# Remaining rows of the experts in blocks of 64 rows, and each tile's results behind its own products

## The chip, the cores and the metric

The kernel runs on one core of one Trainium2 chip, as one launch. The metric is the device time of that launch in microseconds (us), as the median of several executions. The engines are named as in the profile: PE (TensorE) multiplies matrices, PEld is PE's loading of weights, DVE (VectorE) and ACT (ScalarE) work on elements, POOL (GpSimd) here mostly issues indirect DMAs, SP (SyncE) issues plain ones. Work passes between engines through semaphores.

## The reference, cut to what matters

Two layers work on x, of 2 x 2048 tokens with 256 features. The first is a gated linear attention plus a quantised linear map. The second adds, to a normalised input, an attention with 16 heads and a mixture of 8 experts. The change concerns the mixture alone:

```python
logits = xf @ gate_W.T                     # xf: 4096 tokens x 256
pi = _sinkhorn(-logits)                    # 4096 x 8
_, top_idx = jax.lax.top_k(pi, 2)          # two experts for each token
g = jnp.einsum('nd,efd->enf', xf, W_gate)  # 1024 hidden features
u = jnp.einsum('nd,efd->enf', xf, W_up)
y = jnp.einsum('enf,edf->end', jax.nn.silu(g) * u, W_down)
for k in range(2):
    out = out + y[top_idx[:, k], n_ar] * pi[:, k:k + 1]
```

Each token needs only its own two experts, so 8192 pairs of token and expert are to be computed. With the fixed inputs the reference sends 1047, 977, 950, 1003, 1054, 1044, 1029 and 1088 tokens to the eight experts.

## The kernel before, in words

The first layer is worked through in strips of 512 tokens (to about 430 us of the span). Then come the attention of the second layer, with the routing as background work on DVE (to about 894 us), and last the experts' stage.

**Routing.** `Routing.steps` ranks the experts for each token and counts the tokens of each expert. The rows of an expert are laid out in a table in DRAM (`table`) in blocks. `number` is how many whole blocks of 256 rows (`BS`) an expert gets: its count plus 127, divided by 256, rounded down. Where rows remain beyond those, `half` is 1 and the expert gets one block of 128 rows as well. With the counts above each expert gets four whole blocks; three of them don't fill these, and five experts have 23, 30, 20, 5 and 64 rows left, each in a block of 128. `end` sums blocks over the experts, `start` and `away` turn places into rows of the table, `ended`, `expert`, `mine` and `wrow` tell for each block whose it is. `sends` scatters the tokens' rows into the table; rows without a token hold a spare row that adds to a spare part of the output.

**Blocks run.** The program always runs the same list: 32 whole blocks (`FULLS`) and 5 short ones (`HALVES`), the short ones at places 8, 15, 22, 29 and 36 of the 37. If the counts call for more, a flag (`over`, then `c.special` and `c.more`) makes a later branch run all blocks that are not in the list.

**A block** (class `Block`) has these steps:
- `load`: two gathers on POOL (L2146) of the expert's weights, `wgateup` with 2 MB and `wdown` with 1 MB, and one load of its rows on SP's queue (L2162). They are traced two blocks ahead.
- `open_rows`: transposes of the rows on PE into `x_ps` (L2184), a copy to `xT` on ACT (L2188), and three small steps on DVE that take the rows' weights `wt` and the places `to`.
- `hidden`: for each of 8 slices of 128 hidden features, four products into `h_ps` (L2206): the expert's weights, 128 x 128, are the stationary operand and the block's rows the moving one. ACT's silu gives `sg` (L2211), and DVE multiplies it into `hT` (L2212; the profile calls that room `larger`).
- `add_rows`: for each tile of 128 rows 8 products into `y_ps` (L2222): here the rows of `hT` are the stationary operand and 256 columns of `wdown` the moving one. Then, for each tile, DVE multiplies by `wt` and adds half of a bias (L2227; its output `y` appears as `va`), and POOL adds the rows to the output with an indirect DMA (L2231).

All is fp32, and a fp32 product leaves two weight loads and two product records in the trace. The two tiles of a whole block share one PSUM tile of 128 x 512 (`y_ps`, in a pool of one buffer); `h_ps` and `x_ps` draw on seven others.

**Order.** `Experts.pieces` writes the order: for block n the loads of block n+2, `hidden` of n, `open_rows` of n+1, then `add_rows` of n-1. In the last block `add_rows` of the block before stands behind the first quarter of `hidden`. The framework's planner then orders each engine's queue by its own reckoning of when each instruction is ready, with program order as priority. `keep_in_program_order` holds single instructions (the transposes, the row loads, two of the small DVE steps) behind what was traced on their engine before. The framework sets all semaphores.

Of the kernel before, what the change touches and what calls it, by code (L numbers as in the profile page):

```python
# [56 lines left out]
I32 = mybir.dt.int32  # L57
AF = mybir.ActivationFunctionType
ALU = mybir.AluOpType
# [3 lines left out]
P = 128  # L63
B, N, E = 2, 2048, 256
# [18 lines left out]
NE, FF = 8, 1024  # L83
NFC = FF // P
BS = 256
NC = BS // P
NFULL = (2 * B * N + NE * (BS // 2 - 1)) // BS
NHALF = NE
NBLK = NFULL + NHALF
ROWS = NFULL * BS + NHALF * BS // 2  # L90
FULLS, HALVES = 2 * B * N // BS, 5
SPARE = B * N
RW = E + NE + 1
SINKHORN_ITERS = 20
# [121 lines left out]
@with_exitstack  # L216
def two_layers(ctx: ExitStack, tc: tile.TileContext, a: dict, out: bass.AP):
    nc = tc.nc
    const = ctx.enter_context(tc.tile_pool(name="const", bufs=1))

    def load(name, shape, view=None, eng=None, dt=F32):
        t = const.tile(shape, dt, tag=name, name=name)
        (eng or nc.sync).dma_start(out=t, in_=view if view is not None else a[name])
        return t

    c = SimpleNamespace()
    c.ident = load("ident", [P, P])
# [12 lines left out]
    c.wrow = const.tile([P, NBLK], I32, tag="wrow", name="wrow")  # L240
    c.half_bias = const.tile([P, E], F32, tag="half_bias", name="half_bias")

    dram = ctx.enter_context(tc.tile_pool(name="dram", bufs=1, space=bass.MemoryType.DRAM))
    c.table = dram.tile([ROWS, RW], F32, tag="table", name="table")
    c.normed = dram.tile([B * N, E], F32, tag="normed", name="normed")
    c.normed_v = c.normed.rearrange("(t p) e -> p t e", p=P)
    c.qk = dram.tile([2, 2, P, B * N], F32, tag="qk", name="qk")
    c.v = dram.tile([B * N, VW], F32, tag="v", name="v")
    c.x_in = a["x"].rearrange("b n e -> (b n) e").rearrange("(t p) e -> p t e", p=P)
    c.out_v = out[0 : B * N, :].rearrange("(t p) e -> p t e", p=P)  # L250

    blocks = list(range(FULLS))
    for i in range(HALVES):
        blocks.insert(FULLS - 6 * i, NFULL + i)
    usual_way(tc, a, out, c, blocks)

    def where(flag):
        return tc.If(nc.values_load(flag[0:1, 0:1], min_val=0, max_val=1) > 0)

    with where(c.special):  # L260
        with where(c.more):
            layer1_experts(tc, a, out, c, [b for b in range(NBLK) if b not in blocks])
        with where(c.general):
            general_way(tc, a, out, c)
# [35 lines left out]
def general_way(ctx, tc, a, out, c):  # L300
# [16 lines left out]
    nc.vector.memset(c.half_bias, 0.0)  # L317
    layer1_experts(tc, a, out, c, range(NBLK))


class Fill:
# [1603 lines left out]
class Routing:  # L1925
# [3 lines left out]
    def __init__(self, nc, vector, pool, a, c):  # L1929
# [24 lines left out]
    def steps(self, pool, psum, pi):  # L1954
# [5 lines left out]
        nc, vector = self.nc, self.vector  # L1960
# [64 lines left out]
        count = upto[:, NT - 1, :]  # L2025
# [2 lines left out]
        vector.tensor_scalar(number, count, float(BS // 2 - 1), None, ALU.add)  # L2028
        vector.tensor_scalar(number, number, BS.bit_length() - 1, None, ALU.logical_shift_right)
        blocks = tile_("blocks", [P, 2, NE])  # L2030
        full, half = blocks[:, 0, :], blocks[:, 1, :]
        vector.tensor_copy(full, number)
        in_full = tile_("in_full", [P, NE])
        vector.tensor_scalar(in_full, full, float(BS), None, ALU.mult)
        vector.tensor_tensor(half, count, in_full, ALU.is_gt)
        yield
        end = blocks
        for step in (1, 2, 4):
# [5 lines left out]
            end = more  # L2044
# [3 lines left out]
        vector.tensor_scalar(start, start, float(BS), None, ALU.mult)  # L2048

        away = tile_("away", [P, NE])  # L2050
        vector.tensor_tensor(away, end[:, 1, :], half, ALU.subtract)
        vector.scalar_tensor_tensor(away, end[:, 0, :], -2.0, away, ALU.mult, ALU.add)
        vector.tensor_scalar(
            away, away, float(BS // 2), float(NFULL * BS), ALU.mult, ALU.add
        )
        yield
        shape = [P, NT, NE]
# [10 lines left out]
        for to, mark in zip(self.places, (first, second)):  # L2068
            own = tile_("own", [P, NT, NE], tag="sk_beaten")
# [6 lines left out]

        ended = tile_("ended", [P, NBLK, NE], tag="sk_equal")
        for n, bs in enumerate((slice(0, NFULL), slice(NFULL, NBLK))):
# [14 lines left out]
        vector.tensor_scalar(row, expert, float(P), self.pidx, ALU.mult, ALU.add)  # L2093
        vector.tensor_copy(self.c.wrow, row)
        over = self.over
        for n, done in enumerate((FULLS, HALVES)):
            vector.tensor_scalar(
                over[:, n : n + 1], end[0:1, n, NE - 1 :], float(done), None, ALU.is_gt
            )
# [33 lines left out]
class Block:  # L2133


    def __init__(self, e, n, b):
        self.e, self.n, self.b = e, n, b
        self.tiles = NC if b < NFULL else NC // 2
        self.rows = self.tiles * P
        self.first = b * BS if b < NFULL else NFULL * BS + (b - NFULL) * BS // 2  # L2140

    def gather(self, name):

# [14 lines left out]
        self.wd = self.gather("wdown").rearrange("p (c d) -> p c d", c=NFC)  # L2158

    def load_rows(self):  # L2160
        self.xb = self.e.rooms("xb", self.n, [P, NC, RW])[:, 0 : self.tiles, :]
        load = self.e.nc.sync.dma_start(  # L2162
            out=self.xb,
            in_=self.e.c.table[self.first : self.first + self.rows, :].rearrange(
                "(c p) r -> p c r", p=P
            ),
        )
        self.e.tc.keep_in_program_order(load)
# [6 lines left out]
    def open_rows(self):  # L2175


        nc, rooms, n, xb, keep = (
            self.e.nc, self.e.rooms, self.tiles, self.xb, self.e.tc.keep_in_program_order
        )  # L2180
        ps = rooms("x_ps", self.n, [P, 2 * BS]).rearrange("p (e r) -> p e r", e=2)
        for e in range(2):
            for c in range(n):
                keep(nc.tensor.transpose(  # L2184
                    ps[:, e, c * P : (c + 1) * P], xb[:, c, e * P : (e + 1) * P], self.e.c.ident
                ))
        self.xT = rooms("xT", self.n, [P, 2, BS])
        nc.scalar.copy(self.xT[:, :, 0 : self.rows], ps[:, :, 0 : self.rows])  # L2188
        by = rooms("by", self.n, [P, NC, NE])[:, 0:n, :]
        keep(nc.vector.tensor_tensor(  # L2190
            by, xb[:, :, E : E + NE],
            self.e.c.mine[:, self.b : self.b + 1, :].to_broadcast([P, n, NE]), ALU.mult,
        ))
        self.wt = rooms("wt", self.n, [P, NC])
        nc.vector.tensor_reduce(self.wt[:, 0:n], by, AX.X, ALU.add)
        self.to = rooms("to", self.n, [P, NC], I32)
        keep(nc.vector.tensor_copy(self.to[:, 0:n], xb[:, :, E + NE]))

    def hidden(self):
# [14 lines left out]
                yield  # L2214

    def add_rows(self):
        nc, out = self.e.nc, self.e.out
        ps = self.e.rooms("y_ps", self.n, [P, NC * E]).rearrange("p (c d) -> p c d", c=NC)
        y = self.e.rooms("y", self.n, [P, NC, E])
        for c in range(self.tiles):  # L2220
            for fc in range(NFC):
                nc.tensor.matmul(  # L2222
                    ps[:, c, :], lhsT=self.hT[:, fc, c * P : (c + 1) * P], rhs=self.wd[:, fc, :],
                    start=fc == 0, stop=fc == NFC - 1,
                )
        for c in range(self.tiles):
            nc.vector.scalar_tensor_tensor(  # L2227
                y[:, c, :], ps[:, c, :], self.wt[:, c : c + 1], self.e.c.half_bias,
                ALU.mult, ALU.add,
            )  # L2230
            nc.gpsimd.indirect_dma_start(  # L2231
                out=out, out_offset=bass.IndirectOffsetOnAxis(ap=self.to[:, c : c + 1], axis=0),
                in_=y[:, c, :], in_offset=None, compute_op=ALU.add,
            )


# [50 lines left out]
def _constants():  # L2287
    f32 = np.float32
    c = {"ident": np.eye(P, dtype=f32)}
# [21 lines left out]
    to = ((s <= t) * 1 - (s <= 63)).astype(f32)  # L2311
# [3 lines left out]
    own = np.zeros((P, HR), f32)  # L2315
# [4 lines left out]
    c["spare"] = np.zeros((P, RW), f32)  # L2320
    c["spare"][:, E + NE] = SPARE + np.arange(P)
    c["number"] = (np.arange(NT)[None, :, None] * P + np.arange(P)[:, None, None]).astype(f32)
    own = np.concatenate([np.arange(NFULL), np.arange(NHALF)])
    c["bidx"] = np.broadcast_to(own[None, :, None], (P, NBLK, NE)).astype(f32)
    c["eidx"] = np.broadcast_to(np.arange(NE)[None, :], (P, NE)).astype(f32)
    c["before"] = np.tile((np.arange(NE)[None, :] < np.arange(NE)[:, None]).reshape(1, -1), (P, 1)).astype(f32)
# [122 lines left out]
```

## Time and profile before

| | us |
|---|---|
| median of 3 runs | 1642.38 (1642.37 to 1642.56) |
| the profiled execution, its own time | 1642.09 |
| its span in the profile | 1640.3 |
| PE busy | 1583.8 (97%) |
| DVE busy | 730.3 (45%) |
| ACT busy | 743.9 (45%) |
| POOL busy | 391.2 (24%) |
| experts' stage, from the first `h_ps` record | 893.5 to the end |
| mean share of the clock granted to PE | 0.989 |

The span counts from the first to the last profiled instruction; the device time has some 1.8 us more around it. "Busy" is the union of an engine's instructions. The timeline and the chain give starts and lengths in us from the span's start. In the timeline a product's record includes its latency, so that records overlap; the chain shows the time by which each moved the end.

### The profile page before, as it was taken

Reading aid. Unit: us, or ns where it says so; the run is one execution under the profiler, and the core shown is the slowest. Engines: PE = TensorE matmul, PEld = TensorE weight load, DVE = VectorE, ACT = ScalarE, POOL = GpSimd, SP = SyncE. Lnnn points to the kernel's source line nnn. Section 1 sums busy time; section 2 is a strip of 40 time slices with the busy share of each in tenths; the row PEclk is TensorE's granted clock in tenths of the full one; section 3 lists DMA queues with packets and bytes.
Section 4 is the critical chain, followed back from the end, with each engine's and each line's share of the span. In section 5 each row is a group of like instructions: output and inputs, shape, how many; then the busy total and the mean of one; then the engine's idle time right before and its main releaser. Section 6 shows DMA issues by size and latency. Waiting matters only on the chain.

```text
span 1640.3 us, 33123 instructions
## 1 busy us (share of the span) xinstructions
PE 1583.8 (97%) x13786; PEld 1297.9 (79%) x13786; DVE 730.3 (45%) x2274; ACT 743.9 (45%) x1445; POOL 391.2 (24%) x350
## 2 busy tenths in 40 slices
PE   7789999999999999999999999999999999999996
PEld 4556676667688887888888888988898898888886
DVE  7888676664478866444353222222222222222221
ACT  4344554653688888998987211111111111111110
POOL 4333222211200003233331122222222232222221
PEclk9999999999899999999999999999999999999998
DMA  9710111313540402621126555555565565556531
GB/s 268 187 38 29 54 53 43 93 45 80 149 57 3 84 13 66 142 65 62 58 97 246 180 177 177 180 183 174 180 205 198 164 215 195 171 170 196 177 90 19
DMA packets 82511, 204.42 MB, mean 125 GB/s; under 512 B 8624, under 2 KB 64304, under 8 KB 71728
## 3 DMA queue, kind: packets, MB, share of 16 engines
q0 software_dynamic: 24944, 138.33, 26.0%
q1 hardware_dynamic: 56304, 62.71, 14.2%
q8 instruction: 110, 1.80, 0.5%
q10 hardware_dynamic: 1104, 1.18, 0.2%
q14 instruction: 49, 0.40, 0.1%
HBM read 152.26 MB, written 49.92 MB: 123 GB/s over the span
## 4 chain that ended last, share of the span: by engine, by line
PE 86%; DVE 9%; POOL 2%; ACT 1%; DMA 1%; issue 1%; POOLq 0%; SPq 0%; DVEq 0%; ACTq 0%
PE h_ps L2206 29%; PE y_ps L2222 14%; PE sc L1801 12%; PE o_ps L1823 10%; PE vf_ps L533 3%; PE y_ps L533 3%; PE f_ps L1785 2%; PE tr L583 2%; PE vg_ps L533 2%; PE qk_ps L533 1%; PE g_ps L533 1%; PE q_ps L533 1%; PE o_tr L1758 1%; PE o_ds_ps L533 1%; PE x_ps L2184 1%
## 5 line engine op out<-in xcount | busy, mean ns | idle before, releaser
L2206 PE MATMUL h_ps<-va,qk 128*128 128x256 f32 (+1 forms) x2368 | 484.5, 365 | 0.0
L2206 PEld LDWEIGHTS h_ps<-va,qk 128*128 128x128 f32 x2368 | 425.6, 190 | 53.6 <-issue 0.3
L1807 ACT ACTIVATE pt<-sc,shift 128x512 f32<-128x512 f32 (+3 forms) x687 | 403.8, 704 | 52.3 <-ACT pt L1807 27.1
L2211 ACT ACTIVATE sg<-h_ps 128x256 f32<-128x256 f32 (+1 forms) x296 | 109.2, 369 | 600.5 <-PE h_ps L2206 592.9
L2212 DVE TENSOR_TENSOR larger<-sg,h_ps 128x256 f32<-128x256 f32 (+1 forms) x296 | 119.2, 403 | 359.1 <-ACT sg L2211 359.1
L1801 PE MATMUL sc<-qk 32*128 32x128 f32 (+6 forms) x3916 | 222.5, 336 | 1.6 <-PE norm_ps L533 1.1
L1801 PEld LDWEIGHTS sc<-qk 32*128 32x128 f32 x3916 | 184.1, 186 | 35.3 <-ACT pt L1807 17.0
L1823 PE MATMUL o_ps<-pt,va 128*32 128x128 f32 (+6 forms) x3916 | 188.3, 319 | 3.4 <-DVE o_sb L114 3.4
L1823 PEld LDWEIGHTS o_ps<-pt,va 128*32 128x32 f32 x3916 | 140.6, 110 | 34.3 <-issue 9.6
L2231 POOL DMA_INDIRECT out<-va,to x69 | 109.9, 1592 | 211.0 <-DMA out<-va,to 85.4
L114 DVE TENSOR_TENSOR pt<-pt,keepmask 128x128 f32<-128x128 f32 (+3 forms) x546 | 119.7, 276 | 73.7 <-ACT pt L1807 71.8
L2222 PE MATMUL y_ps<-qk,larger 128*128 128x256 f32 x560 | 124.6, 379 | 0.1
L2227 DVE SCALAR_TENSOR_TENSOR va<-y_ps,wt,half_bias 128x256 f32<-128x256 f32 x69 | 30.4, 479 | 208.5 <-PE y_ps L2222 208.5
L2222 PE MATMUL y_ps<-larger 128*128 128x256 f32 x544 | 120.4, 379 | 0.0
L2222 PEld LDWEIGHTS y_ps<-qk,larger 128*128 128x128 f32 x560 | 104.7, 190 | 13.8 <-DVE larger L2212 0.5
L2222 PEld LDWEIGHTS y_ps<-larger 128*128 128x128 f32 x544 | 102.0, 190 | 13.1
L2116 POOL DMA_INDIRECT table<-rows,place x64 | 67.7, 1057 | 186.0 <-DMA table<-rows,place 149.4
L2146 POOL DMA_INDIRECT qk<-in_wgateup,wrow x37 | 36.7, 991 | 190.4 <-PE h_ps L2206 157.7
L533 PE MATMUL vf_ps<-qk,xnT 128*128 128x512 f32 x128 | 59.2, 617 | 0.0
L533 PEld LDWEIGHTS vf_ps<-qk,xnT 128*128 128x128 f32 x128 | 24.4, 196 | 29.6 <-issue 27.3
L114 DVE COPY o_sb<-o_ps 128x256 f32<-128x256 f32 x64 | 26.9, 422 | 42.1 <-PE o_ps L1823 41.8
L2146 POOL DMA_INDIRECT qk<-in_wdown,wrow x19 | 18.4, 968 | 110.2 <-PE y_ps L2222 83.6
(248 smaller groups left out, 1712.2 us busy)
## 6 DMA issues: line engine op xcount, KB each, us to landing
xb<-table SPq DMA_DIRECT2D x32, 265.0 KB
qk<-qk SPq DMA_DIRECT2D x32, 256.0 KB
qk<-qk SPq DMA_DIRECT2D x64, 128.0 KB
table<-spare SPq DMA_DIRECT2D x3, 2120.0 KB
va<-v SPq DMA_DIRECT2D x4, 1208.0 KB
v<-v SPq DMA_DIRECT2D x8, 574.0 KB
normed<-xn SPq DMA_DIRECT2D x8, 512.0 KB
rows<-normed POOLq DMA_DIRECT2D x16, 256.0 KB, 3.3
```

What stands on the lines that cost most here:

```text
L114: return lambda *a, **k: self.tc.keep_in_program_order(begin(*a, **k))
L533: tc.keep_in_program_order(nc.tensor.matmul(*args, **kwargs))
L1801: nc.tensor.matmul(scs[r][:, at : at + q1 - q0], lhsT=heads[rows, 1, kb * P : (kb + 1) * P], rhs=heads[rows, 0, qt * QT + q0 : qt * QT + q ...
L1807: nc.scalar.activation(pt[:, r, 0:width], scs[r][:, 0:width], AF.Exp, bias=shift)
L1823: nc.tensor.matmul(o_ps[r * HR : (r + 1) * HR, to + q0 : to + q1], lhsT=values[b, way][:, kb, h * VC : h * VC + HR], rhs=pt[:, r, at : at ...
L2116: self.nc.gpsimd.indirect_dma_start(out=self.c.table, in_=rows[:, n, :], in_offset=None, out_offset=bass.IndirectOffsetOnAxis(ap=to[:, 2 * ...
L2146: e.nc.gpsimd.indirect_dma_start(out=w, out_offset=None, in_=e.a[name], in_offset=bass.IndirectOffsetOnAxis(ap=e.c.wrow[:, self.b : self.b ...
L2206: nc.tensor.matmul(ps[:, j, rows], lhsT=self.wgu[:, j, c, f * P : (f + 1) * P], rhs=self.xT[:, c, rows], start=c == 0, stop=c == 1,)
L2211: nc.scalar.activation(sg, ps[:, 0, rows], AF.Silu)
L2212: nc.vector.tensor_tensor(self.hT[:, f, rows], sg, ps[:, 1, rows], ALU.mult)
L2222: nc.tensor.matmul(ps[:, c, :], lhsT=self.hT[:, fc, c * P : (c + 1) * P], rhs=self.wd[:, fc, :], start=fc == 0, stop=fc == NFC - 1,)
L2231: nc.gpsimd.indirect_dma_start(out=out, out_offset=bass.IndirectOffsetOnAxis(ap=self.to[:, c : c + 1], axis=0), in_=y[:, c, :], in_offset= ...
```

## The change

Blocks for remaining rows have 64 rows (`SB`) in place of 128, and an expert may have none, one or two of them: `small` is 1 where rows remain, and 2 where more than 64 do. There are up to 16 such blocks in place of 8 (`NBLK` goes from 43 to 51); the list that always runs still has 32 whole blocks and 5 short ones (`SMALLS`). The table has the same number of rows. A short block's tiles take 64 partitions, its transposes, `hidden` and `add_rows` work on 64 rows. In `add_rows` the second loop over the tiles is gone: DVE's step and the scatter of a tile stand behind the tile's own 8 products, ahead of the products of the next tile.

```diff
-NHALF = NE
-NBLK = NFULL + NHALF
-ROWS = NFULL * BS + NHALF * BS // 2
-FULLS, HALVES = 2 * B * N // BS, 5
+SB = 64
+NSMALL = 2 * NE
+NBLK = NFULL + NSMALL
+ROWS = NFULL * BS + NSMALL * SB
+FULLS, SMALLS = 2 * B * N // BS, 5
...
-        vector.tensor_tensor(half, count, in_full, ALU.is_gt)
+        vector.tensor_tensor(small, count, in_full, ALU.is_gt)
+        two = tile_("two", [P, NE])
+        vector.scalar_tensor_tensor(two, in_full, float(SB), count, ALU.add, ALU.is_lt)
+        vector.tensor_tensor(small, small, two, ALU.add)
...
-        vector.tensor_tensor(away, end[:, 1, :], half, ALU.subtract)
-        vector.scalar_tensor_tensor(away, end[:, 0, :], -2.0, away, ALU.mult, ALU.add)
+        vector.tensor_tensor(away, end[:, 1, :], small, ALU.subtract)
+        vector.scalar_tensor_tensor(
+            away, end[:, 0, :], -float(BS // SB), away, ALU.mult, ALU.add
+        )
...
-        self.tiles = NC if b < NFULL else NC // 2
-        self.rows = self.tiles * P
-        self.first = b * BS if b < NFULL else NFULL * BS + (b - NFULL) * BS // 2
+        self.tiles, self.p = (NC, P) if b < NFULL else (1, SB)
+        self.rows = self.tiles * self.p
+        self.first = b * BS if b < NFULL else NFULL * BS + (b - NFULL) * SB
...
                 keep(nc.tensor.transpose(
-                    ps[:, e, c * P : (c + 1) * P], xb[:, c, e * P : (e + 1) * P], self.e.c.ident
+                    ps[:, e, c * P : c * P + p], xb[:, c, e * P : (e + 1) * P],
+                    self.e.c.ident[0:p, 0:p],
                 ))
...
         for c in range(self.tiles):
             for fc in range(NFC):
                 nc.tensor.matmul(
-                    ps[:, c, :], lhsT=self.hT[:, fc, c * P : (c + 1) * P], rhs=self.wd[:, fc, :],
+                    ps[0:p, c, :], lhsT=self.hT[:, fc, c * P : c * P + p], rhs=self.wd[:, fc, :],
                     start=fc == 0, stop=fc == NFC - 1,
                 )
-        for c in range(self.tiles):
             nc.vector.scalar_tensor_tensor(
-                y[:, c, :], ps[:, c, :], self.wt[:, c : c + 1], self.e.c.half_bias,
+                y[0:p, c, :], ps[0:p, c, :], self.wt[:, c : c + 1], self.e.c.half_bias[0:p, :],
                 ALU.mult, ALU.add,
             )
             nc.gpsimd.indirect_dma_start(
                 out=out, out_offset=bass.IndirectOffsetOnAxis(ap=self.to[:, c : c + 1], axis=0),
-                in_=y[:, c, :], in_offset=None, compute_op=ALU.add,
+                in_=y[0:p, c, :], in_offset=None, compute_op=ALU.add,
             )
```

More of the change, by code (lines that the diff above doesn't have):

```diff
@@ L252, in two_layers @@
     blocks = list(range(FULLS))
-    for i in range(HALVES):
+    for i in range(SMALLS):
         blocks.insert(FULLS - 6 * i, NFULL + i)
@@ L2030, in steps @@
         blocks = tile_("blocks", [P, 2, NE])
-        full, half = blocks[:, 0, :], blocks[:, 1, :]
+        full, small = blocks[:, 0, :], blocks[:, 1, :]
         vector.tensor_copy(full, number)
@@ L2050, in steps @@
         away = tile_("away", [P, NE])
-        vector.tensor_tensor(away, end[:, 1, :], half, ALU.subtract)
-        vector.scalar_tensor_tensor(away, end[:, 0, :], -2.0, away, ALU.mult, ALU.add)
+        vector.tensor_tensor(away, end[:, 1, :], small, ALU.subtract)
+        vector.scalar_tensor_tensor(
+            away, end[:, 0, :], -float(BS // SB), away, ALU.mult, ALU.add
+        )
         vector.tensor_scalar(
-            away, away, float(BS // 2), float(NFULL * BS), ALU.mult, ALU.add
+            away, away, float(SB), float(NFULL * BS), ALU.mult, ALU.add
         )
@@ L2095, in steps @@
         over = self.over
-        for n, done in enumerate((FULLS, HALVES)):
+        for n, done in enumerate((FULLS, SMALLS)):
             vector.tensor_scalar(
@@ L2160, in load_rows @@
     def load_rows(self):
-        self.xb = self.e.rooms("xb", self.n, [P, NC, RW])[:, 0 : self.tiles, :]
+        self.xb = self.e.rooms("xb", self.n, [P, NC, RW])[0 : self.p, 0 : self.tiles, :]
         load = self.e.nc.sync.dma_start(
@@ L2164, in load_rows @@
             in_=self.e.c.table[self.first : self.first + self.rows, :].rearrange(
-                "(c p) r -> p c r", p=P
+                "(c p) r -> p c r", p=self.p
             ),
@@ L2175, in open_rows @@
     def open_rows(self):
-        nc, rooms, n, xb, keep = (
-            self.e.nc, self.e.rooms, self.tiles, self.xb, self.e.tc.keep_in_program_order
+        nc, rooms, n, p, xb, keep = (
+            self.e.nc, self.e.rooms, self.tiles, self.p, self.xb, self.e.tc.keep_in_program_order
         )
@@ L2188, in open_rows @@
         nc.scalar.copy(self.xT[:, :, 0 : self.rows], ps[:, :, 0 : self.rows])
-        by = rooms("by", self.n, [P, NC, NE])[:, 0:n, :]
+        by = rooms("by", self.n, [P, NC, NE])[0:p, 0:n, :]
         keep(nc.vector.tensor_tensor(
             by, xb[:, :, E : E + NE],
-            self.e.c.mine[:, self.b : self.b + 1, :].to_broadcast([P, n, NE]), ALU.mult,
+            self.e.c.mine[0:p, self.b : self.b + 1, :].to_broadcast([p, n, NE]), ALU.mult,
         ))
-        self.wt = rooms("wt", self.n, [P, NC])
+        self.wt = rooms("wt", self.n, [P, NC])[0:p, :]
         nc.vector.tensor_reduce(self.wt[:, 0:n], by, AX.X, ALU.add)
-        self.to = rooms("to", self.n, [P, NC], I32)
+        self.to = rooms("to", self.n, [P, NC], I32)[0:p, :]
         keep(nc.vector.tensor_copy(self.to[:, 0:n], xb[:, :, E + NE]))
@@ L2216, in add_rows @@
     def add_rows(self):
-        nc, out = self.e.nc, self.e.out
+        nc, out, p = self.e.nc, self.e.out, self.p
         ps = self.e.rooms("y_ps", self.n, [P, NC * E]).rearrange("p (c d) -> p c d", c=NC)
@@ L2322, in _constants @@
     c["number"] = (np.arange(NT)[None, :, None] * P + np.arange(P)[:, None, None]).astype(f32)
-    own = np.concatenate([np.arange(NFULL), np.arange(NHALF)])
+    own = np.concatenate([np.arange(NFULL), np.arange(NSMALL)])
     c["bidx"] = np.broadcast_to(own[None, :, None], (P, NBLK, NE)).astype(f32)
```

## The prediction

> **What bounds the kernel now.** I read the page first: which engine carries the time, and over which lines the chain that ended last runs.
>
> ```profile
> PE 1583.8 (97%) x13786; PEld 1297.9 (79%) x13786; DVE 730.3 (45%) x2274; ACT 743.9 (45%) x1445; POOL 391.2 (24%) x350
> ...
> PE h_ps L2206 29%; PE y_ps L2222 14%; PE sc L1801 12%; PE o_ps L1823 10%; PE vf_ps L533 3%; PE y_ps L533 3%; PE f_ps L1785 2%; PE tr L583 2%; PE vg_ps L533 2%; PE qk_ps L533 1%; PE g_ps L533 1%; PE q_ps L533 1%; PE o_tr L1758 1%; PE o_ds_ps L533 1%; PE x_ps L2184 1%
> ```
>
> The two products of the experts hold 43% of the chain. The windows of 100 us show that stage without a gap in PE, at the full clock (PE, PEld, DVE, ACT, POOL, then clock, DMA share, GB/s):
>
> ```profile
> 1300.00:1400.00 100.00, 100.00 (x505) 88.94 (x504) 22.62 (x67) 17.84 (x47) 25.72 (x20) 1.00 0.57 185
> ```
>
> So here only PE's own time counts. The chain around one short block (start, length in us) gives its price list:
>
> ```profile
> 1465.56 6.91 PE y_ps L2222 x32
> 1472.47 7.14 PE h_ps L2206 x64
> 1479.61 0.44 PE x_ps L2184 x4
> ...
> 1501.21 3.46 PE y_ps L2222 x16
> ```
>
> A fp32 product leaves two records. A short block's 64 `h_ps` records take 7.14 us, 111.6 ns each, where a whole block's take 13.81 us, 215.8 ns each; its 16 `y_ps` records take 3.46 us, 216 ns each. Five short blocks thus cost PE about 5 x 10.8 = 54 us: that is all the first half of the change can touch.
>
> **The change part by part. Fewer rows in `hidden`.** The five remainders (23, 30, 20, 5 and 64 rows) each fit one block of 64, so five short blocks stay, at half the rows. In `h_ps` the rows are the moving operand: it goes from 128 to 64 columns, but the 64 weights per block stay 128x128. From the two sizes a column costs (215.8 - 111.6)/128 = 0.81 ns, so by columns a record would fall to 59.5 ns, a block by 64 x 52.1 ns = 3.33 us and five by 16.7 us. But every record needs its own weights first. How often can PE take in a weight? The weight rows by form (busy us, mean ns) and, from the timeline, the two records of a product with only 8 moving columns say it:
>
> ```profile
> L2206 PEld LDWEIGHTS h_ps<-va,qk 128*128 128x128 f32 x2368 | 425.6, 190 | 53.6 <-issue 0.3 <-ACT va L2188 0.2
> ...
> L1823 PEld LDWEIGHTS o_ps<-pt,va 128*32 128x32 f32 x3916 | 140.6, 110 | 34.3 <-issue 9.6 <-DVE o_sb L114 3.8 <-DVE pt L114 1.3
> ```
> ```profile
> 445.34 0.39 PE L1556 MATMUL sk_ps<-sk_c,ones_mat 128*128 128x8 f32 x2
> ```
> ```profile
> 445.34 0.30 PEld L1556 LDWEIGHTS sk_ps<-sk_c,ones_mat 128*128 128x128 f32 x2
> ```
>
> 128 weight columns take 190 ns against 110 ns for 32: 80/96 = 0.83 ns for a column, 107 ns for 128, besides a fixed part that overlaps. The two `sk_ps` loads of some 190 ns span 0.30 us, so they begin 0.11 us apart, and the two products, of 0.28 us at most, span 0.39 us: they end 0.11 us apart too. With 8 columns or with 128, a record comes every 0.11 us. The short block already sits on that floor (111.6 ns), and 64 columns lie between 8 and 128. I therefore take 0 for this part; the bounds are 0 and -16.7 us. [...]
>
> In `y_ps` the rows are the weight: 64 columns of weight (about 53 ns less to load) behind 256 moving columns at 216 ns. The load was hidden behind the product already: 0. The transposes keep 128 weight columns: 0. On ACT and DVE the `sg` and `larger` steps get shorter (277 and 287 ns now); both wait for PE, so 0, save some 0.1 us at the very end. The short blocks' row loads and scatters halve; at a DMA share of 0.57 with PE never waiting, also 0.
>
> **The routing.** Two small DVE steps are added (`two`, and one addition), 0.17 us each by their neighbours of 128x8, and `ended`, `expert` and `mine` grow from 43 to 51 blocks, 19% of 0.5 us each. DVE is on the chain only in one stretch of this (from 617 to 631 us), where the wider steps add about 0.3 us. I take +0.3 us, from 0 to 0.8.
>
> **A tile's results behind its own products.** In each of the 32 whole blocks DVE's `va` step (L2227) and the scatter of tile 0 move ahead of the 16 records of tile 1. Both tiles lie in one PSUM tile of 128 x 512 fp32. Does the order matter? The DVE timeline:
>
> ```profile
> 1466.40 0.15 DVE L2197 CAST to<-xb 128x1 int32<-128x1 f32 x1
> 1472.51 0.88 DVE L2227 SCALAR_TENSOR_TENSOR va<-y_ps,wt,half_bias 128x256 f32<-128x256 f32 x2 [5.95 <-PE y_ps L2222]
> ```
>
> Tile 0's products were done at 1465.56 + 3.46 = 1469.02, DVE was idle, and yet it began at 1472.51, right behind the last record of tile 1 (1472.47). Accesses to the two halves are kept apart as if they were one. In the new order this turns round: tile 1's first product must wait until DVE has read tile 0. [...]
>
> Its price: 0.04 us until DVE starts, 0.48 us for the step (its mean in the groups is 479 ns), some 0.05 us back to PE (taken like the way there): 0.57 us, 18.2 us for 32 blocks, if PE stands still. Queued behind it on PE are tile 1's 16 records and the next block's 64 `h_ps` records, and behind those ACT and DVE. But the planner orders each queue by what is ready in its own reckoning, and on PE it has moved products forward before:
>
> ```profile
> 911.44 0.60 PE L2184 MATMUL x_ps<-ident,xb 128*128 128x128 f32 x4
> 911.88 1.03 PE L2222 MATMUL y_ps<-qk,larger 128*128 128x256 f32 x4
> ```
>
> These four `y_ps` records belong, by the program, behind `hidden` of the block that follows; they fill the 0.6 us in which ACT copies `x_ps`. In the new order the next block's `h_ps` products are ready when tile 0 ends (their transposes are 3.46 us old, the copy takes 0.59 us), so I expect two of them (4 records, 0.86 us) in the gap, covering 0.57 us. I take 0 for the wait: the copy of `x_ps` is the nearest row, with almost the same length. The bounds are 0 and 18.2 us; with one product as cover (0.43 us), 0.14 us is left in each block, 4.5 us in all. If anything it is DVE's queue that gains: `va` of tile 0 passes nothing there. On POOL the scatter of tile 0 may now pass the `wdown` gather, which waits for tile 1; that weight is used two blocks later, some 40 us, and lands in 6: 0, and even a wait for a landing scatter (up to 7.8 us) would stay hidden.
>
> **The end.** Here the earlier scatter counts. Scatters into `out` follow one another at 4.5 us, each waiting for the last to land (POOL's timeline, then DVE's last step):
>
> ```profile
> 1620.07 1.56 POOL L2231 DMA_INDIRECT out<-va,to  x1 [2.96 <-DVE va L2227]
> 1624.53 1.56 POOL L2231 DMA_INDIRECT out<-va,to  x1 [2.89 <-DVE larger L2212]
> 1630.04 1.56 POOL L2231 DMA_INDIRECT out<-va,to  x1 [3.96 <-DMA out<-va,to]
> ```
> ```profile
> 1627.79 0.48 DVE L2227 SCALAR_TENSOR_TENSOR va<-y_ps,wt,half_bias 128x256 f32<-128x256 f32 x1 [2.86 <-PE y_ps L2222]
> ```
>
> The last rows were ready at 1628.27 and their scatter waited until 1630.04. With tile 0 of the two blocks before finished 3.46 us sooner, four scatters at a spacing of 4.51 us start at 1607.6 and leave the queue free at 1625.6. Then the last one starts 0.28 us behind its DVE step, at 1628.55: 1.5 us sooner. It has 64 rows in place of 128; for that I add 0.2 us, up to 1.1. What is late next is PE. The end gives -1.7 us, between -0.5 and -2.6.
>
> **The sum.** The profiled execution took 1642.09 us (span 1640.3, 1.8 around it). 0 (`h_ps`) + 0 (covered wait) + 0.3 (routing) - 1.7 (end) = -1.4 us: 1640.7 us, and 0.3 us more against the median of 1642.38: 1641.0 us. A measurement here can tell about 0.2% (3.3 us) from no change.
>
> **The rivals.** *The wait is not covered* (slower): PE stands still in the 32 whole blocks. For it: `h_ps` of the next block comes after both tiles in the program, and what the planner reckons need not be what the chip takes. Against it: the 911.88 row. Price 18.2 - 1.4: 1659 us. It decides as soon as more than 0.15 us is left open in a block. *Cover of one product*: 4.5 - 1.4, 1645.5 us. *Time follows rows*: 16.7 us less, 1624 us; against it the `sk_ps` rows. *The clock falls*: with 64 columns PE streams 53 of 111.6 ns, 48%. The windows show the clock behind a thin stretch of PE work:
>
> ```profile
> 136.20:139.61 3.41, 1.47 (x14) 1.23 (x13) 2.25 (x13) 0.84 (x2) 1.01 (x1) 1.00 0.00 0
> 139.61:143.02 3.41, 3.41 (x8) 1.59 (x6) 3.38 (x8) 0.58 (x1) 0.00 (x0) 0.50 0.85 294
> 214.70:218.12 3.42, 1.70 (x10) 1.17 (x10) 3.39 (x13) 0.00 (x0) 1.26 (x1) 1.00 0.00 0
> ```
>
> 1.47 of 3.41 us (43%) was followed by 3.4 us at 0.50; after 1.70 of 3.42 (50%) the clock stayed. 48% is nearer to the second. If it falls, two such stretches for a short block lose 1.7 us each, 17 us in all: 1658 us. *More blocks than foreseen*: the last expert's remainder is 64 exactly; one row more makes a sixth short block, and the 14 blocks not in the list run as well, 3 of some 21 us and 11 of some 11: over 1800 us. The inputs give 64, so this is nearly out.
>
> **How the numbers follow.** My forecast 0.57; wait uncovered 0.14; one product as cover 0.13; rows 0.09; clock 0.05; more blocks 0.02. The forecast's own range is 1639 to 1643. To hold 8 in 10 the range must reach to the uncovered wait: 1639 to 1660, leaving out rows, more blocks and the outer edges. Faster by over 0.2%: rows and 0.06 of the forecast (a larger gain at the end), 0.15. Slower: uncovered, clock, more blocks, half of the one-product case and 0.02 of the forecast, 0.29. Within: 0.56.
>
> **What would show it.** Right: short blocks' `h_ps` x64 again at 7.1 us; `y_ps` x16, a few `h_ps` records, `y_ps` x16 on PE; L2227 one at a time, 3.5 us and more apart; the last scatter at about 1628.5. Wrong: `h_ps` x64 near 3.8 us; PE's idle time put down to `va` near 18 us; a clock below 1.00 beyond 900 us.

## The result and the profile after

The changed kernel took 1645.36 us (median of 12 runs, 1642.39 to 1647.61), the kernel before, run beside it, 1642.55 us (12 runs, 1642.10 to 1646.11). The ratio is 1.0002 with a 95% interval of 0.9992 to 1.0012: no change that can be told. The medians, 2.8 us apart, lie further apart than the ratio says: the runs of both kernels fall into groups some 3 us apart, which arise ahead of the experts' stage (see the fourth block of experiments). So the accounts below are made inside the stage: from the first `h_ps` record to the end of the last `y_ps` record ("PE's stretch"), and from there to the end of the span ("the tail"), both worked out from the trace's records.

| kernel | PE's stretch | tail | sum, us |
|---|---|---|---|
| before | 734.23 | 12.55 | 746.78 |
| changed | 736.70 | 10.32 | 747.02 |

In a second profile of before the tail is 12.34 us, 0.21 less, so the 0.24 us in the sum can't be told from nothing. But the sum holds two larger parts of opposite sign. The page of the changed kernel (busy time of each engine, then shares of the chain) and its window of 100 us look like the ones before:

```profile
PE 1588.7 (97%) x13786; PEld 1291.3 (79%) x13786; DVE 730.7 (44%) x2276; ACT 741.4 (45%) x1445; POOL 388.2 (24%) x350
...
PE h_ps L2213 29%; PE y_ps L2229 15%; PE sc L1802 12%; PE o_ps L1824 10%; PE y_ps L534 3%; PE vf_ps L534 2%; PE f_ps L1786 2%; PE qk_ps L534 2%; PE vg_ps L534 2%; PE tr L584 2%; PE g_ps L534 1%; PE o_tr L1759 1%; PE q_ps L534 1%; PE o_ds_ps L534 1%; PE x_ps L2190 1%
```
```profile
1300.00:1400.00 100.00, 100.00 (x503) 87.25 (x502) 22.11 (x67) 17.69 (x48) 25.52 (x20) 1.00 0.58 193
```

PE is still without a gap and at the full clock. The chain around the same short block as in the prediction (start, length in us) shows where the stage's time is:

```profile
1469.89 0.27 PE x_ps L2190 x2
1470.15 3.65 PE y_ps L2229 x16
1473.80 1.28 PE h_ps L2213 x12
1475.09 3.51 PE y_ps L2229 x16
1478.60 5.75 PE h_ps L2213 x52
1484.35 0.44 PE x_ps L2190 x4
1484.79 3.46 PE y_ps L2229 x16
1488.24 0.86 PE h_ps L2213 x4
1489.11 3.45 PE y_ps L2229 x16
...
1505.95 3.60 PE y_ps L2229 x16
1509.55 14.01 PE h_ps L2213 x64
```

Two rows of before to compare with, besides those in the prediction (the transposes of a short block, and `hidden` of the block behind it):

```profile
1465.34 0.22 PE x_ps L2184 x2
1504.66 13.81 PE h_ps L2206 x64
```

Three things are to be seen. The planner has put products of the next block between the two tiles: 4 records of 256 columns (0.86 us) ahead of a whole block, 12 of 64 columns (1.28 us) ahead of a short one; no gap is left. The short block's 64 `h_ps` records take 1.28 + 5.75 = 7.03 us, against 7.14 with twice the rows. And some groups have grown: `y_ps` x16 behind the transposes of 64 rows 3.65 us (3.46 before), the short block's own `y_ps` 3.60 us (3.46), the `h_ps` x64 behind it 14.01 us (13.81). With 0.05 for the transposes, 0.05 for the group at 3.51 and 0.11 saved in `h_ps`, a short block costs 0.52 us more. Five of them, the last without a block behind it but with two more groups of 3.51 us around it, come to some 2.5 us; PE's stretch grew by 2.47 us.

The tail, in POOL's timeline and DVE's last step:

```profile
1622.50 1.55 POOL L2237 DMA_INDIRECT out<-va,to  x1 [3.24 <-DVE va L2233]
1627.29 1.55 POOL L2237 DMA_INDIRECT out<-va,to  x1 [3.24 <-DVE va L2233]
1633.95 1.42 POOL L2237 DMA_INDIRECT out<-va,to  x1 [5.11 <-DVE va L2233]
```
```profile
1633.20 0.48 DVE L2233 SCALAR_TENSOR_TENSOR va<-y_ps,wt,half_bias 64x256 f32<-64x256 f32 x1 [3.12 <-PE y_ps L2229]
```

The last scatter no longer waits for a landing but for its own DVE step, 0.27 us behind it. From the end of the last product to that scatter it is now 0.79 us, before 2.29: 1.50 us won. From the scatter to the end of the span it is 9.53 us, before 10.26, with half the rows: 0.73 us won (over all profiles 9.16 to 9.60 us with 64 rows and 10.14 to 10.37 with 128). The sum is 2.47 - 1.50 - 0.73 = +0.24 us, the table's difference.

### The profile page after: what moved, and what is told of

Same layout as the page of the kernel before. It is cut to its first block, busy times and chain, and to the rows that moved or that the text cites. A ratio compares the mean times of both kernels' runs of the same rounds, so it can differ in the third digit from the quotient of the medians.

```text
span 1643.5 us, 33122 instructions
## 1 busy us (share of the span) xinstructions
PE 1588.7 (97%) x13786; PEld 1291.3 (79%) x13786; DVE 730.7 (44%) x2276; ACT 741.4 (45%) x1445; POOL 388.2 (24%) x350
## 4 chain that ended last, share of the span: by engine, by line
PE 86%; DVE 9%; POOL 2%; ACT 1%; issue 1%; DMA 0%; SPq 0%; POOLq 0%; another core or an unknown queue 0%; DVEq 0%; ACTq 0%
PE h_ps L2213 29%; PE y_ps L2229 15%; PE sc L1802 12%; PE o_ps L1824 10%; PE y_ps L534 3%; PE vf_ps L534 2%; PE f_ps L1786 2%; PE qk_ps L534 2%; PE vg_ps L534 2%; PE tr L584 2%; PE g_ps L534 1%; PE o_tr L1759 1%; PE q_ps L534 1%; PE o_ds_ps L534 1%; PE x_ps L2190 1%
## 5 line engine op out<-in xcount | busy, mean ns | idle before, releaser
L2213 PE MATMUL h_ps<-va,qk 128*128 128x256 f32 (+1 forms) x2368 | 489.4, 365 | 0.0
L2233 DVE SCALAR_TENSOR_TENSOR va<-y_ps,wt,half_bias 128x256 f32<-128x256 f32 (+1 forms) x69 | 33.4, 483 | 221.1 <-PE y_ps L2229 221.1
L2229 PE MATMUL y_ps<-qk,larger 128*128 128x256 f32 (+1 forms) x560 | 127.7, 380 | 0.1
L2229 PE MATMUL y_ps<-larger 128*128 128x256 f32 (+1 forms) x544 | 123.7, 380 | 0.0
L2229 PEld LDWEIGHTS y_ps<-qk,larger 128*128 128x128 f32 (+1 forms) x560 | 101.1, 185 | 17.3 <-DVE larger L2219 0.5
L2229 PEld LDWEIGHTS y_ps<-larger 128*128 128x128 f32 (+1 forms) x544 | 99.2, 187 | 15.7 <-issue 0.3
L209 POOL TENSOR_TENSOR mx_r<-mx_r,mx_pw 128x512 f32<-128x512 f32 x17 | 22.2, 1307 | 76.3 <-DVE mx_r L208 76.3
```

The lines of the kernel that those rows point to most:

```text
L2213: nc.tensor.matmul(ps[:, j, rows], lhsT=self.wgu[:, j, c, f * P : (f + 1) * P], rhs=self.xT[:, c, rows], start=c == 0, stop=c == 1,)
L2229: nc.tensor.matmul(ps[0:p, c, :], lhsT=self.hT[:, fc, c * P : c * P + p], rhs=self.wd[:, fc, :], start=fc == 0, stop=fc == NFC - 1,)
```

## The experiments

My theory after the first profile of the changed kernel: the floor of weight loads holds `h_ps`, the wait is real but covered, and PE loses about 0.5 us per short block where it passes between its whole array and a part of it (transposes of 64 rows, weights of 64 columns). The main rival: the loss comes from the new order of 32 whole blocks.

**1. The two halves apart.** Order alone: the kernel before with the second loop of `add_rows` merged into the first.

```diff
-        for c in range(self.tiles):
             nc.vector.scalar_tensor_tensor(
```

> Only the second half of the change: short blocks keep 128 rows, but a tile's DVE step and scatter stand behind its own products. Measured from the first h_ps record of the experts' stage to the end of the last y_ps record, PE took 734.2 us before and 736.6 us after. Theory (short blocks of 64 rows lose about 0.5 us each where PE passes between its whole array and a part of it; the wait for the shared bank is covered): 734.2 us again, the last scatter follows its own DVE step, and the time is 1.5 us below the kernel before, 1640.7 to 1641 where before takes 1642.4. Rival (the loss comes from the new order, 0.08 us in each of 32 whole blocks): 736.7 us, and 1 us above before.

Measured: 1642.14 us, ratio 0.9991 (0.9980 to 1.0002); PE's stretch 735.29 us, tail 11.16 us. The tail fell by 1.39 us as expected, but PE's stretch grew by 1.06 us, which neither theory had. The chain ahead of a short block, here with 128 columns, shows it:

```profile
1195.73 0.67 PE h_ps L2206 x6
1196.40 3.63 PE y_ps L2222 x16
```

Only 6 records, 0.67 us, stand between the tiles, and the second tile takes 3.63 us in place of 3.46. This happens six times (once ahead of four short blocks, twice around the last): 6 x 0.17 = 1.0 us. The cover there is too short; how long it has to be, run 2 says.

Rows alone: the changed kernel with the two loops of before in `add_rows`.

```diff
+        for c in range(self.tiles):
             nc.vector.scalar_tensor_tensor(
                 y[0:p, c, :], ps[0:p, c, :], self.wt[:, c : c + 1], self.e.c.half_bias[0:p, :],
```

> Only the first half: short blocks of 64 rows, both tiles' results behind both tiles' products as before. Theory: PE's stretch takes 736.6 us, h_ps x64 of a short block 7.0 us, and the last scatter still waits for the landing of the one before; 2 to 2.5 us above before, less some 0.4 us for a scatter of half the rows. Rival (loss from the order): 734.2 us and about 0.4 us below before.

Measured: 1644.82 us, ratio 1.0008 (0.9997 to 1.0018); PE's stretch 736.70 us, the changed kernel's to the hundredth, tail 11.14 us. So in the changed kernel all of PE's loss comes with the rows; the order costs PE something only where the short blocks keep 128 rows. The tail fell by 1.4 us without the order, more than I expected: 1.1 us of it lies behind the last scatter (9.16 us against 10.26), 0.3 ahead of it, where the scatter still waits for a landing. The short block's own `y_ps` and the `h_ps` behind it have the lengths that they have in the changed kernel:

```profile
1227.15 3.60 PE y_ps L2229 x16
1230.75 14.01 PE h_ps L2213 x64
```

**2. The wait for the shared PSUM tile** (`y_ps`; the expectations say bank). First without cover: every `h_ps` product from the fourth block on is held in program order.

```diff
-                    nc.tensor.matmul(
+                    product = nc.tensor.matmul(
...
+                    if self.n >= 3:
+                        self.e.tc.keep_in_program_order(product)
```

> The changed kernel, with every h_ps product from the fourth block on held behind all products traced before it, so that nothing can stand between the two tiles' y_ps products. Theory (the second tile waits for DVE's read of the shared bank, and two h_ps products cover it): PE stands still about 0.57 us in each of 31 whole blocks, 17.7 us in all, put down to va; the time is about 1660 us. Rival (there is no wait, or it is much shorter): within 3 us of the changed kernel.

Measured in one run: 1667.94 us where before took 1643.46; PE's stretch 762.90 us, 26.2 us more than in the changed kernel. The chain in a whole block:

```profile
1214.80 3.47 PE y_ps L2231 x16
1218.27 0.02 issue
1218.30 0.49 DVE va L2235
1218.79 0.04 issue
1218.83 3.72 PE y_ps L2231 x16
```

PE stands still for 0.56 us, which is the 0.57 us of the prediction, and then the second tile takes 3.72 us in place of 3.45: after a stop, PE needs 0.27 us more to be under way again. The records show where: the first product and the load of its weights both begin at 1218.83 and the product's record lasts 0.48 us, while each later one moves the end by only 0.22. Uncovered, a wait costs 0.83 us, and 31 of them 25.7 us, nearly all of the 26.2; the 17.7 us that I expected were too few by the restarts. So 4 records of 256 columns (0.86 us) are just enough; 6 records of 128 columns (0.67 us) leave 0.16 us, the 0.17 us seen with the order alone.

Then without the wait: the second tile's products in another PSUM tile.

```diff
+        sums = [
+            self.e.rooms(name, self.n, [P, NC * E]).rearrange("p (c d) -> p c d", c=NC)
+            for name in ("y_ps", "x_ps")[0 : self.tiles]
+        ]
...
         for c in range(self.tiles):
+            ps = sums[c]
```

> The changed kernel, with the second tile's products in another PSUM bank (one of the seven that h_ps and x_ps share), so that no product waits for DVE. Theory (the wait is fully covered already): no h_ps records between the two tiles' y_ps records, PE's stretch 736.6 us as in the changed kernel within 0.5 us, same time. Rival (each whole block still pays a bit for the interleaving, some 0.08 us): 734 us, 2.5 us faster than the changed kernel.

```profile
1209.16 3.46 PE y_ps L2233 x16
1212.62 3.45 PE x_ps L2233 x16
1216.07 13.81 PE h_ps L2213 x64
```

Nothing stands between the tiles any more (the second one's room is now called `x_ps`), and PE's stretch is 736.70 us, as in the changed kernel; the tail 10.39 us. The time was 1646.32 us, ratio 1.0010 (1.0001 to 1.0019), the excess lying ahead of the stage. The wait was covered in full; the rival, a small price in each whole block, is out.

**3. What sets `h_ps`, and what the short blocks lose.** Whole array: short blocks of 128 rows, new order, but only 64 moving columns in `hidden`.

```diff
-        nc, rooms, rows = self.e.nc, self.e.rooms, slice(0, self.rows)
+        nc, rooms, rows = self.e.nc, self.e.rooms, slice(0, BS if self.b < NFULL else 64)
...
-        for c in range(self.tiles):
             nc.vector.scalar_tensor_tensor(
```

> Short blocks of 128 rows as before, with the new order; but in hidden a short block's products take only its first 64 rows as moving columns (the other rows, all spare here, keep old values of hT). So transposes and y_ps products use all 128 partitions and 128 weight columns, and only the moving side has 64 columns. Theory (the loss of 0.5 us per short block comes from transposes of 64 rows and from weights of 64 columns): no loss, h_ps x64 7.0 us, PE's stretch 734 us, time like the order alone, 1.5 us below before. Rival (64 moving columns themselves bring the loss): 736.6 us and the time of the changed kernel.

Measured: 1640.24 us, ratio 0.9985 (0.9976 to 0.9995); PE's stretch 734.05 us, tail 11.13 us. The 64 moving columns bring no loss in all. The short block's `y_ps` and the `h_ps` behind it have their old lengths again (only the 3.51 us of the tile behind 12 narrow records stays, and with it the 0.11 us saved in `h_ps`):

```profile
1224.53 3.46 PE y_ps L2222 x16
1227.98 13.81 PE h_ps L2206 x64
```

It is also better than the order alone, since 12 records of 64 columns cover the wait (1.28 us) where 6 of 128 did not. Both are 768 columns, so the planner seems to count by columns, and narrow products as shorter than PE takes for them.

Eight columns: the changed kernel with only 8 moving columns.

```diff
+        nc, rooms, rows = self.e.nc, self.e.rooms, slice(0, BS if self.b < NFULL else 8)
```

> The changed kernel, with only 8 of a short block's 64 rows as moving columns of h_ps (the other rows of hT keep old values, so the results of those rows are left out). Theory (a record waits for its 128 weight columns): h_ps x64 of a short block still 6.9 to 7.1 us, the time as changed. Rival (time follows the moving columns, 0.81 ns each over a small fixed part): about 1 us for x64, 30 us less in all.

Measured in one run: 1667.67 us, PE's stretch 761.53 us. Windows in a short block (busy us of PE, PEld, DVE, ACT, POOL; then PE's clock, DMA share, GB/s):

```profile
1197.00:1200.00 3.00, 3.00 (x27) 2.92 (x25) 0.81 (x3) 0.35 (x2) 1.48 (x1) 1.00 0.92 385
...
1204.00:1208.00 4.00, 4.00 (x15) 3.55 (x16) 0.16 (x1) 0.18 (x1) 0.00 (x0) 0.50 0.00 0
```

At the full clock 27 records take 3 us, 0.11 us each, with 8 columns as with 64 and 128: the floor is there. But both theories missed what follows: a few us into each of the five short blocks the clock falls to 0.50, for 6.8 us in the first and 10.2 us in the others. By an estimate, these 47.8 us at half the clock lose 23.9, of the 24.8 us by which the stretch grew over the changed kernel's. That is the prediction's rival of the falling clock, at 8 columns; at 64 the changed kernel's clock stayed at 1.00 from 424 us on to the end of PE's work.

Half weights: the changed kernel with 64 of the 128 weight columns of each `h_ps` product in short blocks.

```diff
+        w = P if self.b < NFULL else 64
...
-                        ps[:, j, rows], lhsT=self.wgu[:, j, c, f * P : (f + 1) * P],
+                        ps[0:w, j, rows], lhsT=self.wgu[:, j, c, f * P : f * P + w],
```

> The changed kernel, with only 64 of the 128 weight columns of each h_ps product in short blocks (half of the hidden features are left out there), and all 64 rows moving. Theory (a weight column costs 0.83 ns): 55 to 60 ns a record, x64 3.6 us, 17 us less in all but for 1 us of passing between part and whole of the array. Rival (a fixed cost per record of 0.11 us): 7.0 us, no change.

Measured in one run: 1631.34 us, PE's stretch 723.43 us, 13.3 us less than in the changed kernel, where the theory had some 16. The 64 records of a short block took 4.02 us in place of 7.03.

```profile
1198.45 3.25 PE L2214 MATMUL h_ps<-va,qk 128*64 128x64 f32 x52
```

52 records in 3.25 us are 61 ns each (the last one's latency left out), against 110 ns for the same 64 moving columns and 128 weight columns. Twice the weights, nearly twice the time: the weight columns set the pace. The prediction's estimate of 0.83 ns for a weight column gives 107 ns for 128 columns and 53 for 64. The spacing of the records in these runs agrees, with 3 to 8 ns on top; the record of one load is longer (190 ns in the prediction's row, 136 ns with 64 columns in the `a_ps` rows of before), as loads overlap.

**4. A version that keeps the blocks of 64, and the groups of runs.** Blocks of 64 with the whole array: transposes take all 128 partitions of the row buffer and `y_ps` all 128 columns of `hT`; what doesn't belong to the block isn't read on.

```diff
+        self.whole = self.e.rooms("xb", self.n, [P, NC, RW])
+        self.xb = self.whole[0 : self.p, 0 : self.tiles, :]
...
-                    ps[:, e, c * P : c * P + p], xb[:, c, e * P : (e + 1) * P],
-                    self.e.c.ident[0:p, 0:p],
+                    ps[:, e, c * P : (c + 1) * P], self.whole[:, c, e * P : (e + 1) * P],
+                    self.e.c.ident,
...
-                    ps[0:p, c, :], lhsT=self.hT[:, fc, c * P : c * P + p], rhs=self.wd[:, fc, :],
+                    ps[:, c, :], lhsT=self.hT[:, fc, c * P : (c + 1) * P], rhs=self.wd[:, fc, :],
```

> The changed kernel with blocks of 64 rows kept, but PE's array is never used in part: a short block's transposes take all 128 partitions of the row buffer (64 of them old rows) and its y_ps products all 128 columns of hT (64 of them old); only the 64 rows that belong to it are read on. Theory (passing between whole and part of the array costs 0.5 us per short block): PE's stretch from the first h_ps record to the end of the last y_ps record falls from 736.7 to 734.1 us, the span behind that stretch stays 10.3 us, and the time is 2.6 us below the changed kernel, 2 below before. Rival (the loss comes with 64 rows in a block in some other way): 736.7 us as in the changed kernel.

Measured: PE's stretch 734.05 us, tail 10.06 us, 744.11 us together, 2.67 us below before: both parts as expected. The chain at the end of a short block:

```profile
1222.16 3.46 PE y_ps L2230 x16
1225.62 13.81 PE h_ps L2214 x64
```

Where a passage costs its time can be read from single records. In the changed kernel, the load of the first `h_ps` weights behind a short block's `y_ps`, and its product:

```profile
1509.47 0.30 PEld L2213 LDWEIGHTS h_ps<-va,qk 128*128 128x128 f32 x2 [0.39 <-issue]
1509.48 0.48 PE L2213 MATMUL h_ps<-va,qk 128*128 128x256 f32 x1
```

The same place with the whole array:

```profile
1225.24 0.41 PEld L2214 LDWEIGHTS h_ps<-va,qk 128*128 128x128 f32 x2
1225.45 0.38 PE L2214 MATMUL h_ps<-va,qk 128*128 128x256 f32 x1
```

With the whole array the load begins 0.21 us ahead of its product, while the product before it runs. At the passage it begins only with its product, and the product takes 0.48 us in place of 0.38. At the other two large passages load and product also begin together (1470.08 and 1505.88 us). All records behind such a first one end 0.216 us apart, as before, the short block's own `y_ps` records with 64 weight columns too. So the price lies in the passage, not in working on a part of the array. The four passages around a short block cost 0.05 (into the transposes), 0.19, 0.14 and 0.20 us; five blocks, the last without the fourth passage, make 2.7 us, and the two kernels differ by 2.65.

The timing as a whole doesn't show the gain: 1639.22 us against 1638.96 for before on the same chip, ratio 0.9997 (0.9987 to 1.0007), since there the groups of runs are wider apart than the gain. They go with the mean clock granted to PE in a run. The 29 runs of before on this chip split by it without exception: 1637.16 to 1639.18 us at 0.991 or more (16 runs), 1641.36 to 1643.14 at 0.990 or less (13 runs). At the higher clock this kernel took 1636.6 us on average (4 runs) and before 1638.5; at the lower clock 1640.1 (8 runs) and 1642.3. That is some 2 us less on either side, as expected; but this comparison was chosen after the runs.

Second gather later: in the changed kernel, the second of two weight gathers that run during the attention is issued 20 steps later.

```diff
             for block in ahead:
                 block.load_rows()
-                block.load_gate_up()
+            ahead[0].load_gate_up()
+        if n == len(units) - 12:
+            ahead[1].load_gate_up()
```

> The changed kernel with the second of the two weight gathers that run during the attention issued 20 steps later. In the changed kernel's profile a fetch of instructions comes every 7 us, but none between 842.0 and 853.3 us, while the two gathers of 4 MB run; ACT and PE lose some 2 us there. Theory (the fetch waits behind the gathers, and that sets the groups of times 1642.5 and 1645 to 1647): with 2 MB at a time the late fetch stays within its lead, most runs lie in the lower group, the median is about 2.5 us below the changed kernel's. Rival (the groups have another cause): median and spread as the changed kernel.

Both together:

> Both of the above together, as a version that may beat both kernels: if both theories hold, 2.6 us below the changed kernel by PE's stretch and 2.5 us by the median of the attention's stage, about 1640 us where before takes 1642.5 to 1643.4. If only the array counts, as the run with the whole array alone.

And the kernel before once more:

> The kernel before, unchanged, for a second profile. Theory (a late fetch of instructions during the gathers makes the difference between groups of runs, whatever the kernel): if its time is above 1643.5 us, the time is lost between 830 and 870 us, in a gap between fetches of over 10 us, and the experts' stage is the same 746.8 us; if it is below, no such loss. Rival: the difference lies elsewhere, in the experts' stage or at the start.

Measured: the later gather 1641.81 us, ratio 1.0006 (0.9996 to 1.0015); both together 1639.30 us, ratio 0.9988 (0.9978 to 0.9999), stage 744.40 us; before again, one run, 1642.14 us with a stage of 746.57 us, without the loss at the gathers, as expected for a run below 1643.5 us. But on this chip 1642.14 us belongs to the upper of the two groups, so here that loss does not make the groups. What does is not settled. One part of it can be seen at the start of the attention: in some runs the clock is at 0.50 for 6.8 us, in others for 3.4. The windows there, of before again and of the blocks of 64 with the whole array (9 us each, the second 2 us earlier because that run was earlier by as much):

```profile
435.00:444.00 9.00, 8.49 (x108) 6.91 (x111) 5.21 (x20) 7.68 (x13) 7.64 (x5) 0.62 0.95 273
```
```profile
433.00:442.00 9.00, 8.49 (x146) 7.34 (x143) 5.47 (x21) 8.36 (x15) 7.70 (x5) 0.81 0.96 271
```

The first `sc` record of the attention came at 434.8 us in the run with the lower clock and at 432.5 in the other, the 600th at 504.8 and 501.1: 1.4 us were lost between them. Another part lies later in the attention. From the 600th `sc` record to the first `h_ps` record it is 388.85 us in both profiles of before, 388.90 to 389.06 in the three profiles with the changed routing in this block of runs, but 392.87 in the changed kernel's profile and 390.8 to 393.7 in the seven runs of blocks 1 to 3 (on two other chips), two of which have the routing of before. In the changed kernel's profile that time is lost around 846 us, while the gathers run and no instructions are fetched for 11.2 us, from 842.0 to 853.3. But the blocks of 64 with the whole array show no loss either, without the later gather, so the later gather could not be tested here. A pause in the fetches alone does not mean a loss: in the first profile of before it is 10.8 us, from 854.9 to 865.7, beside the gathers. From 815 us on, the longest pause is 9.4 to 10.8 us in the five profiles without the loss and 11.5 to 12.4 in the eight with it; which brings about which is open. That the fetch is the cause is argued, not shown.

## Why the prediction was right, and where not

The forecast was no change that can be measured, 1641.0 us in a range of 1639 to 1660, and that is the result (1645.36, ratio 1.0002). Two things in this are luck. In the stage a loss of 2.47 us that was not foreseen and a gain of 2.23 us at the end happen to cancel. And the median lies outside the 1639 to 1643 us that the forecast gave for itself, by time that is lost ahead of the stage (in the profile the first `h_ps` record came 2.9 us later than before), of which the routing, the only step there, makes 0.2 us at most; the whole range holds it only because that reached up to a wait without cover. By its steps:

- **`h_ps`, 0 us.** Right: 7.03 us in place of 7.14, 0.11 us a record with 8, 64 and 128 moving columns, 61 ns with half the weights. The `sk_ps` rows had shown the floor.
- **`y_ps` and transposes of short blocks, 0 us.** This step failed. A record still takes 0.216 us and its load is hidden, but not at the first record behind a passage between the whole array and a part: there the load begins with its product. That made 0.52 us per short block, 2.47 us in all, gone in both runs that use the whole array. The trace of before has no such passage among the short blocks, but the prediction's own `sk_ps` rows held a sign of it: right behind products with 32 weight columns, load and product both begin at 445.34.
- **The wait, 0 us.** Right in mechanism and sign: with both tiles in one PSUM tile and nothing between them the second waited for DVE's read of the first (0.56 us), in two PSUM tiles it didn't, and the planner filled the gap with two products of the next block. The price without cover was mis-sized: 0.83 us in place of 0.57, because PE also needs 0.27 us to get under way again (3.72 us in place of 3.45); that rival would have cost 26 us, not 18. That the cover (0.86 us) still sufficed was luck too.
- **The routing, +0.3 us.** 0.05 to 0.2 us by the runs without the loss in the attention.
- **The end, -1.7 us.** The order's part, 1.5 us, came out as 1.50. The smaller scatter was put at 0.2 us, up to 1.1, and brought 0.73 (1.1 in the run of the rows alone).
- **The sum.** -1.4 us forecast, +0.24 us in the stage and some 0.1 us in the routing measured: the missing 2.5 us of the short blocks, less the scatter's 0.5.
- **The clock.** It stayed at 1.00 with 64 columns and fell to 0.50 with 8. The prediction had set a streaming share (48%) beside shares of busy time (43 and 50%), which are not the same measure; where between 8 and 64 columns the clock falls is open.

## What to carry to other kernels

With fp32 and 128 weight columns for each product, fewer than 128 moving columns bought no time here (0.11 us a record with 128, 64 and 8): look at the rate of weight loads, for example at two neighbouring products with few columns, before cutting rows. When a product writes a PSUM tile that another engine still reads, ask how long the planner's filling lasts on the chip, stop and restart included (0.56 and 0.27 us here), not only that something fills it. And a smaller tile that uses part of PE's array may cost its neighbours more than it saves (0.52 us more for a short block here): look whether the first load behind it still runs ahead of its product. Running the whole array over old data was free here (PE's stretch 734.05 us, before 734.23).

## What the runs showed of the hardware that I had not expected

Passing between whole and part of PE's array cost 0.14 to 0.20 us at three of the four passages around a short block (3.65 and 3.60 us in place of 3.46, 14.01 in place of 13.81), because the first load behind it no longer ran 0.21 us ahead of its product. A stop of PE cost 0.27 us beyond its length (3.72 us in place of 3.45). And PE's clock fell to 0.50 while records followed one another 0.11 us apart, with 8 moving columns behind 128 weight columns, and stayed at 1.00 with 64: PE was busy without a gap in both (3.00 of 3.00 us ahead of the fall, 5.70 of 5.70 with 64), so being busy was not enough, and what differs between the two kernels is the number of moving columns.
